# Attention and feed-forward stack on one core: a list scheduler in place of hand-written time tables, with other score, softmax and norm steps

## The chip, the cores and the metric

The kernel runs on one NeuronCore of a Trainium2 chip. The metric is device time in microseconds: the median of three runs. The profile is one further execution, taken by the hardware profiler. The engines are PE (TensorE; PEld is its weight load), DVE (VectorE), ACT (ScalarE), POOL (GpSimd) and SP (SyncE, which here issues DMAs).

## What is computed

The input x holds 32 batch elements of 128 tokens by 128 channels, all in float32. First comes one cross attention with a residual, then a layer norm, then six layers of local attention and gated feed forward; the sum of the two residual streams is the output. Shortened from the reference:

```
x = x + xattn(layernorm(x), ctx, ...)          # 16 heads of 8, 4 key/value groups, time bias
y = layernorm(x)
for i in range(6):
    # attention: 16 heads of 64; queries and keys are normalised per head, then rotated
    q, k, v = split(shift_tokens(y) @ Wqkv[i])
    q, k = rotate(l2norm(q) * qs), rotate(l2norm(k) * ks)
    y = local_attention(q, k, v) @ Wo[i] + y    # windows of 32, each sees itself and the one before
    # feed forward: layer norm, 341 hidden columns, gelu gate
    t = layernorm(shift_tokens(y)) * g + b
    a, gate = split(t @ W1[i] + b1[i])
    y = (a * gelu(gate)) @ W2[i] + b2[i] + y
return x + y
```

`shift_tokens` delays the upper 64 channels by one token. `layernorm` and `l2norm` need a reciprocal square root per row.

## The kernel before

All activations stay on the chip. Four batch elements form a group (8 groups); one batch element in one layer is a **unit** (192 units). Products that must be precise are made from operands split into a high and a low part, three matmuls into one PSUM bank (`split3`, lines 636 to 638).

A unit makes four 512-wide query and key products (`pqk`). From each bank ScalarE takes squares (line 686), VectorE sums them per head (line 689), and VectorE multiplies the bank by two rotation tables (two instructions, line 694); GpSimd adds the two with halves swapped (line 700). One reciprocal square root over all 32 heads follows: a floor, logarithm and exponential on ScalarE (lines 126, 128), and a Newton step of three instructions; the floor (line 118) and the Newton step (lines 133, 135, 137) run on VectorE. GpSimd applies it (line 723). PE transposes the result (line 729); ScalarE, and VectorE for a part (line 744), copy it out, keys into tiles `kb` whose other half is zero, so that two heads share one matmul over all 128 rows.

Values are multiplied by the product of value and output weights (`py`); ScalarE copies them out (line 762) and four DMAs per product (line 769, 16 a unit) regroup them by window into `ysh`. Scores start with a matmul that writes the mask into the bank (line 781), then 32 logical matmuls (line 786; each is two in the trace). VectorE takes row maxima (line 793). ScalarE makes 16 exponentials of 64 columns a unit, each with its own bias and a sum of its row (line 804; the sum is read out by a second instruction). GpSimd divides (line 813), VectorE transposes in blocks (line 817), and 28 logical matmuls multiply by `ysh` (line 830; 56 in the trace).

Per group: the input is transposed, with a shifting matmul for the upper half (lines 660, 661), and split (lines 666, 670). After attention come a residual, a DMA that shifts the upper half (line 851), statistics in eight instructions of 64 (lines 857, 858), a reciprocal square root on VectorE and ScalarE (lines 116 to 137), and normalising in two GpSimd passes (lines 867, 868 and 880). Then come a transpose, the gate and value products, gelu, their product (line 928), the second product (line 935) and a residual (line 939).

In cross attention each batch element has four groups of heads: scores (line 516), sum with the bias and maximum on VectorE (line 522), subtraction on GpSimd (line 526), exponential (line 530), transposes (line 416), copies (line 537), and one value product per group into a strip of 32 rows (line 542).

What sets the order is written out by hand. Every step is pushed into a heap with a time, and the heap is emptied in order of time; each engine then runs its instructions in that order. The times are the tables `OFF`, `GOFF`, `OFF1` and `GOFF1` times a slot, the same for every group. PSUM has five banks for products, two for scores and one for outputs.

Of the kernel before, what the change touches and what calls it, by code (L numbers as in the profile page):

```python
# [22 lines left out]
NRT = 8  # L23
NYT = 4
NKB = 3
NQT = 3
EWD = (1,)
STORE = 0.4
MP1 = [23.0 + 1.2 * i for i in range(8)]
WV1, DH1, DL1 = [20.85, 22.05], 0.15, 0.3  # L30
PREP0, PREPT = 10.0, 7.0
SHIFT = 6.0
FFT = 7.0
MP = [31.47, 31.72, 31.97, 32.22, 32.47, 32.72, 32.97, 33.22]
WV, BIAS, DH, DL = [24.4, 25.4], 16.4, 0.06, 0.14
T1 = 7.0
NI1 = 180
OFF1 = dict(
    sc=[[0, 2, 26, 28], [32, 34, 73, 75], [93, 95, 139, 141], [154, 159, 170, 172]],
    mx=[[1, 3, 27, 29], [33, 35, 74, 76], [94, 96, 140, 142], [158, 164, 171, 173]],  # L40
    sb=[[4, 5, 30, 31], [36, 37, 77, 78], [97, 98, 143, 144], [165, 168, 174, 175]],
    ex=[[39, 41, 44, 48], [99, 100, 101, 102], [151, 152, 155, 160], [187, 189, 192, 196]],
    tp=[[42, 46, 51, 55], [126, 127, 128, 129], [153, 157, 163, 167], [190, 194, 199, 203]],
    st=[[45, 50, 54, 57], [130, 132, 134, 135], [156, 162, 178, 179], [193, 198, 202, 205]],
    pa=[[49, 53, 82, 83], [131, 133, 136, 137], [161, 166, 186, 188], [197, 201, 218, 220]],
    oT=[[84], [138], [191], [223]], pb=[[145], [146], [195], [227]], rl=[[147], [148], [200], [232]],
    at=[[149], [150], [204], [236]],
)
GOFF1 = dict(
    ldc=[-101], gst=[-121, -120], gr0=[-119], gr1=[-117, -116], gr2=[-115, -114, -113], xa=[-118], xb=[-112],  # L50
    px=[-89], pxe=[-88], pcx=[-100], pce=[-99], pk=[-77], ke=[-76], kd=[-75], pq=[-74, -73, -71, -67],
    qe=[-72, -69, -65, -62], qd=[-70, -66, -63, -60], pv=[-55], vt=[-11], td=[-110], ab=[-109, -108], ln=[-4],
    mkb=[-56], tbm=[-3], p2=[238], aT=[249], pw=[265], rs=[266], hst=[267, 268], hr0=[269], hr1=[292, 296],
    hr2=[299, 301, 302], xf1=[270], xf2=[303],
)
T = 13.3
NI = 331
OFF = dict(
    qk=[[0, 1, 30, 31], [79, 80, 107, 108], [153, 154, 194, 195], [244, 245, 284, 285]],
    sq=[[2, 6, 32, 36], [81, 85, 109, 113], [155, 159, 196, 200], [246, 250, 286, 290]],  # L60
    ss=[[7, 11, 37, 41], [86, 90, 114, 118], [160, 164, 201, 205], [251, 255, 291, 295]],
    ta=[[3, 8, 33, 38], [82, 87, 110, 115], [156, 161, 197, 202], [247, 252, 287, 292]],
    tb=[[4, 9, 34, 39], [83, 88, 111, 116], [157, 162, 198, 203], [248, 253, 288, 293]],
    add=[[5, 10, 35, 40], [84, 89, 112, 117], [158, 163, 199, 204], [249, 254, 289, 294]],
    rs0=[[42], [119], [206], [296]], rs1=[[62, 63], [141, 142], [219, 220], [313, 314]],
    rs2=[[64, 65, 66], [143, 144, 145], [221, 222, 223], [315, 316, 317]],
    mul=[[67, 68, 69, 70], [146, 147, 148, 149], [224, 225, 226, 227], [318, 319, 320, 321]],
    tq=[[100, 102, 104, 136], [181, 183, 185, 228], [268, 270, 272, 275], [354, 356, 358, 381]],
# [15 lines left out]
)  # L84

@with_exitstack
def body(ctx: ExitStack, tc: tile.TileContext, x, ctx_in, fside, mask, xWq, xWk, xWv, xWo, xtw,
         Wqkv, q_scale, k_scale, Wo, ln_g, ln_b, W1, b1, W2, b2, cst, x1d, out):
    nc = tc.nc
    B = x.shape[0]  # L90
# [265 lines left out]
    def attn_ops(g, j, G):  # L356
# [26 lines left out]
        def rs1(c):  # L383
            rsqrt_b(G["rsq"], c)
# [651 lines left out]
```

## Time and profile before

| | us |
|---|---|
| median of three runs | 3325.82 |
| lowest and highest | 3324.84, 3329.13 |
| span of the profiled execution | 3320.9 |

The granted TensorE clock of the profiled execution averages 0.994. Busy time of an engine is the union of its instructions. In lists of groups, a row gives the line, engine, operation, tiles, shapes and count, then busy microseconds and the mean nanoseconds of one, then the engine's idle time before these instructions and what ended it. More rows of that list:

| line | engine, what | count | busy us | mean ns |
|---|---|---|---|---|
| 118 | DVE floor of the per-unit norm | 192 | 164.6 | 857 |
| 133 | DVE first Newton product, per unit | 192 | 94.2 | 491 |
| 135 | DVE second, per unit | 192 | 50.6 | 264 |
| 137 | DVE third, per unit | 192 | 36.9 | 192 |
| 116 | DVE epsilon of the feed-forward norm | 48 | 36.2 | 755 |
| 133 | DVE first Newton product of that norm | 48 | 9.1 | 190 |
| 137 | DVE third Newton product of that norm | 48 | 18.5 | 386 |
| 857, 858 | DVE statistics of 64 columns | 384 | 79.3 | 207 |
| 700 | POOL addition of the rotation | 768 | 980.3 | 1286 |
| 723 | POOL product with the norm | 768 | 777.4 | 1043 |
| 867, 868 | POOL subtraction of the mean | 96 | 59.2 | 616 |
| 880 | POOL product with the feed-forward norm | 48 | 50.0 | 1041 |
| 735 | ACT copy of 128x512 from PSUM | 384 | 208.1 | 590 |
| 739, 746 | ACT copies of 64x512 from PSUM | 576 | 336.9 | 585 |
| 781 | PE mask into the score bank | 384 | 148.7 | 387 |
| 786 | PE scores | 12288 | 375.1 | 262 |
| 660, 661 | PE input transposes and shifts | 576 | 139.3 | 296 |
| 885 | PE transposes for the feed forward | 192 | 30.9 | 284 |

### The profile page before, as it was taken

To read this page: it belongs to the slowest core of one execution; us is meant where nothing else is said; L and a number is where in the kernel's file an instruction comes from. 1 tells how busy PE (TensorE), PEld (TensorE's weight loads), DVE (VectorE), ACT (ScalarE), POOL (GpSimd) and SP (SyncE) were. 2 spreads that over 40 slices of the span, in tenths; PEclk is the share of its full clock that TensorE was granted. 3 is DMA by queue.
4 is the path that set the end of the run, shared out by engine and by line. 5 is a ranking of instruction groups with operands and counts; after the bars stand their busy time and mean duration, and the time that the engine had idled before them with its cause. 6 is when DMAs were issued, how large, how long until landed. Compare 5 with 4: busy or idle time off the path is not lost.

```text
span 3320.9 us, 102077 instructions
## 1 busy us (share of the span) xinstructions
PE 3155.8 (95%) x35979; PEld 2389.3 (72%) x35979; DVE 2979.5 (90%) x6954; ACT 2834.9 (85%) x9983; POOL 2468.3 (74%) x2284
## 2 busy tenths in 40 slices
PE   8999899999999999999999999999999999999997
PEld 5555677777777777777777777777777777777775
DVE  6666899999999999999999998998999998999995
ACT  6776888898888898889898889898888898898895
POOL 5655777777787777787787787786787776777873
PEclk9999999999999999999999999999999999999998
DMA  2110333332333332233332333332333332333332
GB/s 61 33 37 12 77 87 82 79 74 71 75 83 86 78 74 72 72 85 84 77 77 71 75 83 81 79 77 68 79 83 76 84 76 64 77 82 81 82 83 62
DMA packets 217966, 243.80 MB, mean 73 GB/s; under 512 B 83534, under 2 KB 112498, under 8 KB 217458
## 3 DMA queue, kind: packets, MB, share of 16 engines
q1 hardware_dynamic: 217026, 236.93, 28.8%
q8 instruction: 288, 4.72, 0.6%
q14 instruction: 220, 1.80, 0.2%
q10 hardware_dynamic: 432, 0.34, 0.0%
HBM read 25.31 MB, written 4.19 MB: 9 GB/s over the span
## 4 chain that ended last, share of the span: by engine, by line
PE 49%; DVE 32%; ACT 8%; issue 4%; DMA 3%; SPq 2%; POOL 1%; ACTq 0%; DVEq 0%; POOLq 0%
DVE t L694 10%; PE pO L830 8%; PE ptq L729 7%; DVE ss L689 6%; PE sc L786 4%; DVE rnv L118 3%; PE pa L542 3%; PE pqk L636 3%; PE pqk L638 3%; ACT pr L804 3%; PE pqk L637 3%; DVE mx L793 2%; DVE PT L817 2%; SPq L769 2%; PE py L636 2%
## 5 line engine op out<-in xcount | busy, mean ns | idle before, releaser
L700 POOL TENSOR_TENSOR rt<-t,t 128x512 f32<-128x512 f32 x768 | 980.3, 1286 | 372.8 <-DVE t L694 330.8
L694 DVE TENSOR_TENSOR t<-pqk,tab 128x512 f32<-128x512 f32 x1536 | 983.3, 681 | 115.9 <-ACT sq L686 110.3
L804 ACT ACTIVATE pr<-sc,mx 128x64 f32<-128x64 f32 x3072 | 915.7, 331 | 61.2 <-DVE PT L817 53.0
L723 POOL TENSOR_TENSOR rt<-rt,rny 128x512 f32<-128x512 f32 x768 | 777.4, 1043 | 214.1 <-DVE rny L137 213.4
L804 ACT ACTIVATION_READ_ACCUMULATOR pr<-sc,mx 128x1 f32 x3072 | 691.9, 225 | 0.0
L689 DVE TENSOR_REDUCE ss<-sq 128x8 f32<-128x512 f32 x768 | 517.4, 674 | 0.0
L830 PE MATMUL pO<-ysh,PT 128*32 128x128 f32 x10752 | 416.9, 275 | 53.3 <-DVE PT L817 48.7
L813 POOL TENSOR_TENSOR pr<-pr,rl 128x512 f32<-128x512 f32 x384 | 400.8, 1044 | 89.2 <-DVE rl L809 89.2
L686 ACT ACTIVATE sq<-pqk 128x512 f32<-128x512 f32 x768 | 429.3, 600 | 24.6 <-PE pqk L638 12.5
L830 PEld LDWEIGHTS pO<-ysh,PT 128*32 128x32 f32 x10752 | 367.1, 110 | 97.6 <-DVE PT L817 72.1
L762 ACT COPY yt<-py 128x512 f32<-128x512 f32 x768 | 416.8, 614 | 21.2 <-PE py L638 17.2
L729 PE MATMUL ptq<-cs,rt 128*128 128x128 f32 x3072 | 409.8, 278 | 22.2 <-DVE t L694 17.0
L729 PEld LDWEIGHTS ptq<-cs,rt 128*128 128x128 f32 x3072 | 334.5, 141 | 96.7 <-issue 52.5
L786 PE MATMUL sc<-kb,qT 128*32 128x128 f32 (+1 forms) x12288 | 375.1, 262 | 15.2 <-DVE kb L744 14.8
L786 PEld LDWEIGHTS sc<-kb,qT 128*32 128x32 f32 x12288 | 270.7, 109 | 114.5 <-issue 70.7
L636 PE MATMUL py<-mw,xsh 128*128 128x512 f32 x768 | 333.1, 434 | 8.9 <-ACT yt L762 5.8
L636 PE MATMUL pqk<-wqh,xsh 128*128 128x512 f32 x768 | 314.0, 409 | 4.8 <-ACT yt L762 2.8
L638 PE MATMUL py<-mw,xsl 128*128 128x512 f32 x768 | 301.9, 393 | 0.0
L638 PE MATMUL pqk<-wqh,xsl 128*128 128x512 f32 x768 | 300.9, 392 | 0.0
L637 PE MATMUL pqk<-wql,xsh 128*128 128x512 f32 x768 | 300.8, 392 | 0.0
L637 PE MATMUL py<-mw,xsh 128*128 128x512 f32 x768 | 300.6, 391 | 0.0
L735 ACT COPY qT<-ptq 128x512 f32<-128x512 f32 x384 | 208.1, 590 | 79.0 <-PE ptq L729 78.1
(168 smaller groups left out, 5756.8 us busy)
## 6 DMA issues: line engine op xcount, KB each, us to landing
ysh<-yt SPq DMA_DIRECT2D x3072, 64.0 KB
raw<-in_L_ffn_Wqkv SPq DMA_DIRECT2D x36, 256.0 KB
xsu<-xt SPq DMA_DIRECT2D x48, 127.0 KB
wor<-in_L_ffn_Wo SPq DMA_DIRECT2D x6, 512.0 KB
xt<-in_x SPq DMA_DIRECT2D x8, 256.0 KB
cx<-in_ctx SPq DMA_DIRECT2D x8, 256.0 KB
mk<-in_mask_BxS_ff SPq DMA_DIRECT2D x8, 256.0 KB
x_scratch<-xt SPq DMA_DIRECT2D x8, 256.0 KB
```

The lines of the kernel that those rows point to most:

```text
L636: nc.tensor.matmul(pt, lh, rh, start=True, stop=False)
L637: nc.tensor.matmul(pt, lh, rl, start=False, stop=False)
L638: nc.tensor.matmul(pt, ll, rh, start=False, stop=True)
L686: nc.scalar.activation(V["sq", c], V["pp", c], AF.Square)
L689: nc.vector.tensor_reduce(V["ss"][:, c * 8:(c + 1) * 8], V["sq", c].rearrange("p (h d) -> p h d", d=64), axis=AX.X, op=ALU.add)
L694: nc.vector.tensor_tensor(V["t", k, c].rearrange("p h s d -> p h (s d)"), V["pp", c].rearrange("p (h d) -> p h d", d=64), w["tab"][:, c // ...
L700: nc.gpsimd.tensor_tensor(V["rt", c], V["t", 0, c], V["t", 1, c][:, :, ::-1, :], op=ALU.add)
L723: nc.gpsimd.tensor_tensor(rv, rv, V["rn"][:, c * 8:(c + 1) * 8].unsqueeze(2).to_broadcast([P, 8, 64]), op=ALU.mult)
L729: nc.tensor.transpose(V["ptq", c][:, k, :], V["rt", c][:, 2 * k:2 * k + 2].rearrange("p h s d -> p (h s d)"), ident)
L786: nc.tensor.matmul(sc[32 * c:32 * c + 32, :, wd, lo:64], qT[:, c, 32 * wd:32 * wd + 32], kT[:, c, :, 32 * wd - 32 + lo:32 * wd + 32], star ...
L804: nc.scalar.activation(pr[:, q, :], scv[:, q, :], AF.Exp, bias=mx[:, q:q + 1], accum_out=ls[:, q:q + 1])
L830: nc.tensor.matmul(pO[32 * wd:32 * wd + 32, j, :], PT[:, half, wd, blk, :], ysh[u][:, (2 * par + half) * P:(2 * par + half + 1) * P], star ...
```

## The change

The whole body is rewritten around a list scheduler; the mathematics stays the same.

- **Order.** `Sched.op` records a step with its engine (from `COST`), the buffers that it reads and writes, and a priority: the unit's position, plus a correction by name (`LATER`). `Sched.run` plays these steps through with the two durations of `COST` (how long the engine is taken, when the result is there): at each moment each engine takes the ready step of the highest priority whose buffers are free; some steps must leave PSUM banks free (`KEEP`). The instructions are then issued in that order. Cross attention has priorities before those of layer 0. Some pools of buffers hand out their buffers in the order of the program.
- **Scores.** Keys and queries keep both heads of a pair in one tile. Each head has its own matmul over 64 rows, into one of two banks by the half of the rows: 64 logical matmuls, of 32 output rows by 64 columns (32 in the first window). The mask comes into each bank as a ScalarE copy.
- **Softmax.** The negative maxima are added into the bank by one matmul with the identity and a broadcast operand (`fold`); then come one exponential of 512 a bank without bias, a row-sum reduction on VectorE, and the rest as before.
- **Rotation.** One VectorE product of 1024 with both tables replaces two of 512.
- **Norms.** The per-unit floor and Newton step are on VectorE. The epsilon and the Newton step of the layer norms are on GpSimd, in four instructions after the exponential. Normalising in the feed forward is four VectorE instructions with two per-row scalars.
- **Shift.** x is kept with a shifted copy of its upper half beside it, renewed by two DMAs after each residual. Input transposes read it, without shifting matmuls; statistics are four instructions of 128.
- **Cross attention.** The four value products of a batch element are issued together.
- **Value products of a unit** are issued together, once both halves of the softmax are there.

```
-OFF = dict(
-    qk=[[0, 1, 30, 31], [79, 80, 107, 108], [153, 154, 194, 195], [244, 245, 284, 285]],
...
-    def drain():
-        while heap:
-            _, _, fn, a = heapq.heappop(heap)
-            fn(*a)
+COST = dict(
+    ax=("PE", .46, .7), axh=("ACT", .51, .62), axl=("DVE", .60, .68),
...
+    def run(self):
...
+                for o in cand[e]:
+                    if o.ready > t + 1e-9:
+                        continue
+                    if o.table == "E" and hold:
+                        continue
...
+                cand[e].remove(o)
...
+                free[e] = t + occ
...
+        for (_, o), new in zip(order, fresh):
...
+            o.fn()
...
-                nc.tensor.matmul(sc.rearrange("p a b c -> p (a b c)"), identb, maskb, start=True, stop=True)
...
-                for c in range(4):
-                    nc.tensor.matmul(sc[32 * c:32 * c + 32, :, wd, lo:64], qT[:, c, 32 * wd:32 * wd + 32],
-                                     kT[:, c, :, 32 * wd - 32 + lo:32 * wd + 32], start=False, stop=True,
-                                     skip_group_check=True)
+                    for c in range(4):
+                        for a in range(2):
+                            r = slice(64 * a, 64 * a + 64)
+                            nc.tensor.matmul(s4[a][32 * c:32 * c + 32, half, wd, lo:64],
+                                             q[r, c * P + 32 * wd:c * P + 32 * wd + 32],
+                                             k[r, c * P + 32 * wd - 32 + lo:c * P + 32 * wd + 32], start=False, stop=True,
+                                             skip_group_check=True)
+        for a, b in enumerate(sc):
+            S.op("msk", lambda b=b: nc.scalar.copy(b.t, mask), pri, (), [b], k=a)
+        S.op("sc", scores, pri, [*qT, *sc], sc)
...
-            for q in range(4 * half, 4 * half + 4):
-                nc.scalar.activation(pr[:, q, :], scv[:, q, :], AF.Exp, bias=mx[:, q:q + 1],
-                                     accum_out=ls[:, q:q + 1])
+            S.op("fold", lambda: nc.tensor.matmul(s.t, identr, mx.t.unsqueeze(2).to_broadcast([P, 8, 64]), start=False,
+                                                  stop=True, skip_group_check=True), pri, [mx, s], [s], k=a)
+            S.op("ex", lambda: nc.scalar.activation(pr.t, s.t, AF.Exp), pri, [s], [pr], table="E", k=a)
+            S.op("sm", lambda: nc.vector.tensor_reduce(sm.t, r8(pr), axis=AX.X, op=ALU.add), pri, [pr], [sm], k=a)
...
-            nc.vector.tensor_tensor(V["t", k, c].rearrange("p h s d -> p h (s d)"),
-                                    V["pp", c].rearrange("p (h d) -> p h d", d=64),
-                                    w["tab"][:, c // 2, k, :].unsqueeze(1).to_broadcast([P, 8, 64]), op=ALU.mult)
+                nc.vector.tensor_tensor(t.t.rearrange("p (k h d) -> p k h d", k=2, d=64),
+                                        bc(pp.t.rearrange("p (h d) -> p h d", d=64), 2),
+                                        tab.t[:, c // 2].unsqueeze(2).to_broadcast([P, 2, 8, 64]), op=ALU.mult)
...
+        small = NW == "dve" and floor is not None
+        e = nc.vector if small else nc.gpsimd
...
+                    nc.vector.tensor_scalar(xn.t[:, k * P:(k + 1) * P], xsg(g)[:, k], mv.t[:, k, 0:1], r.t[:, k:k + 1],
+                                            op0=ALU.subtract, op1=ALU.mult)
...
+            nc.sync.dma_start(xt[g][1:113, :, 128:192], xt[g][0:112, :, 0:64])
+            nc.sync.dma_start(xt[g][113:P, :, 128:192], xt[g][112:P - 1, :, 0:64])
...
+        def xpa():
+            for h in range(4):
+                nc.tensor.matmul(pa.t[32 * h:32 * h + 32, :], v.t[:, j, h, :], sts[h].t, start=True, stop=True)
```

## The prediction

> **What bounds the kernel now.** I read the busy times first, then the stages, then VectorE's waits, then rows.
>
> ```profile
> PE 3155.8 (95%) x35979; PEld 2389.3 (72%) x35979; DVE 2979.5 (90%) x6954; ACT 2834.9 (85%) x9983; POOL 2468.3 (74%) x2284
> PE 49%; DVE 32%; ACT 8%; issue 4%; DMA 3%; SPq 2%; POOL 1%; ACTq 0%; DVEq 0%; POOLq 0%
> ```
>
> No engine is alone at its limit, and the chain of waits changes hands between PE and DVE, so the shares must be read by stage. The columns of the stage view are start:end, length, then busy time and instructions of PE, PEld, DVE, ACT and POOL. The first two lines are cross attention and one whole layer; the third is that layer again with line 830 alone (columns PE and PEld).
>
> ```profile
> 40.00:300.00 260.00, 247.17 (x1589) 144.38 (x1588) 172.99 (x1177) 185.12 (x376) 148.94 (x142) 1.00 0.11 31
> 1326.40:1820.70 494.30, 476.22 (x5704) 369.06 (x5701) 462.31 (x933) 437.23 (x1594) 381.05 (x351) 1.00 0.32 78
> 1326.40:1820.70 494.30, 68.80 (x1795) 60.64 (x1792) 1.00 0.32 78
> ```
>
> A unit (one batch element in one layer) issues 56 matmuls at line 830, so 1792 are 32 units: 494.3 / 32 = 15.45 us a unit, and 192 x 15.45 = 2966 us. The first query matmul of layer 0 starts at 299.5 us in the timeline. Of the span of 3320.9 us, 300 is thus cross attention, 2966 the layers, and 55 filling and draining. PE's 96% in a layer counts the modelled ends of pipelined matmuls; VectorE, in order, is busy 462.3 / 494.3 = 93.5%, 14.45 us a unit. I take it as the bound of the layers. Its idle 32.0 us of that layer:
>
> ```profile
> DVE t L694 <- ACT sq L686: 16.9, 24, 2.8
> DVE u L928 <- PE pa L638: 5.0, 14, 0.4
> ```
>
> Half of the idle time ends on ScalarE, which is itself busy 437.2 / 494.3 = 88%. Some of VectorE's busy time is no work:
>
> ```profile
> 1502.53 1.29 POOL L700 TENSOR_TENSOR rt<-t,t 128x512 f32<-128x512 f32 x1 [0.49 <-PE ptq L729]
> 1503.01 0.84 DVE L118 TENSOR_SCALAR rnv<-ss 128x32 f32<-128x32 f32 x1
> 1503.77 0.19 DVE L809 RECIPROCAL rl<-ls 128x8 f32<-128x8 f32 x1
> ```
>
> The 32-element step of line 118 takes 0.84 us and ends where the GpSimd instruction ends (1503.82). Its shortest instance takes 0.235. Such steps, SBUF to SBUF on VectorE, sit out a running GpSimd instruction.
>
> **The change, by engine, per unit of a layer.** The rows (count over the execution | busy us, mean ns):
>
> ```profile
> L694 DVE TENSOR_TENSOR t<-pqk,tab 128x512 f32<-128x512 f32 x1536 | 983.3, 681 | 115.9 <-ACT sq L686 110.3 <-POOL pr L813 1.6 <-POOL rt L700 0.9
> L689 DVE TENSOR_REDUCE ss<-sq 128x8 f32<-128x512 f32 x768 | 517.4, 674 | 0.0
> L744 DVE COPY kb<-ptq 64x512 f32<-64x512 f32 x192 | 133.4, 695 | 7.0 <-ACT kb L739 1.0
> L135 DVE SCALAR_TENSOR_TENSOR frt<-frv,frt 128x4 f32<-128x4 f32 x48 | 43.8, 912 | 1.6
> L804 ACT ACTIVATE pr<-sc,mx 128x64 f32<-128x64 f32 x3072 | 915.7, 331 | 61.2 <-DVE PT L817 53.0 <-DVE mx L793 0.9
> ```
>
> *VectorE.* Two products of 512 become one of 1024: now 8 x 0.64 = 5.12 us. The 128-wide score step of line 522 (0.286) and the 512-wide one here (0.681) give 1.03 ns an element, so 4 x (0.64 + 512 x 1.03 ns) = 4.67: -0.45. The copy of line 744 goes: -0.70. The row sums that ScalarE's accumulator made become two reductions like line 689: +2 x 0.674 = +1.35. The four steps of the feed-forward norm (36.2 + 9.1 + 43.8 + 18.5 = 107.6 us over 192 units) leave for GpSimd: -0.56. Eight statistics steps of 64 (79.3 us) become four of 128 (0.280 each, line 374): 0.28 - 0.41 = -0.13. Normalising comes from GpSimd as four steps of 128x128 a group; line 334 has that shape at 0.223 with GpSimd idle: 4 x 0.223 / 4 = 0.22. Their wait for GpSimd is not in this trace. Least is none; most is a whole 1.29 us addition each, 1.29 a unit. The nearest row is the old norm: four steps, 107.6 / 48 = 2.24 us a group; the shortest of lines 116, 133 and 137 are 0.17, 0.12 and 0.16, and with 0.16 for the fourth, work is 0.6, so 1.64 of waits a group, 0.41 a unit, which I take: +0.63 in all. The per-unit norm is on VectorE before (lines 118 to 137, 346 us, 1.80 a unit) and after: 0, at best -1.0 (their shortest instances, 0.235 + 0.146 + 0.191 + 0.191 = 0.76), at worst +0.45 (as long as the old norm's 2.24). Sum: 14.45 - 0.45 - 0.70 + 1.35 - 0.56 - 0.13 + 0.63 = **14.59 us**, from 13.1 to 15.9. VectorE's load hardly moves.
>
> The Trainium skill (SBUF — State Buffer, "SBUF: two separate sides") makes this wait a lock on a port pair held for a whole instruction, also against VectorE instructions in a two-port mode. By it all four normalising steps lose what is left of an addition; at a whole one each VectorE would carry 15.47 us a unit and, filled like my forecast, the kernel would take 3372 us. The row of the old norm, with 0.41 us per step lost on average (1.64 / 4), says 3198.
>
> *ScalarE.* 16 exponentials of 64 with their accumulator reads go: they start some 0.29 apart in the timeline, -4.6. Two of 512 (line 530, 0.628) and two mask copies (line 735, 0.59) come: +2.44. Five evacuations of transposes become four: -0.48. 13.66 becomes 11.0: the largest relief, off VectorE's chain except where VectorE waited for the square.
>
> *PE.* The mask matmuls go, 148.7 / 192 = -0.77; two 512-wide folds come, 0.23 each by the start times of lines 637 and 638 (1502.92, 1503.15): +0.46. Input transposes lose the shifting matmuls: (83.1 + 56.2 - 30.9) / 192 = -0.56. Scores: 64 matmuls (1.95 us) become 128, half as tall, half as wide. The timeline up to 1509.18 and up to 1509.31:
>
> ```profile
> 1509.15 0.26 PE L786 MATMUL sc<-kb,qT 128*32 128x64 f32 x4
> 1509.15 0.43 PE L786 MATMUL sc<-kb,qT 128*32 128x64 f32 x12
> ```
>
> Four column strips start together and the next four 64-wide ones 0.065 us on. If the row halves overlap too: 16 x 0.065 + 0.27 = 1.3 us. If not: 32 x 0.065 + 0.27 = 2.35. I take 1.8. PE: 14.88 falls by 1.5 to 0.5; at my value to 13.9, below VectorE either way.
>
> A rule of the Trainium skill (TensorE: Matmul & The Clock Gate, "Wait — 56ns, not 53.3ns?") speaks against this: matmul starts are never nearer than about 25 ns, however narrow. By it 128 cost 3.2 us, PE 15.26 a unit, 15.73 at the same fill, and the kernel 3330 us instead of 3198. But the row has eight starts in 0.13 us, 16 ns each, so across strips the row decides.
>
> *GpSimd.* 381.1 / 32 = 11.9; two normalising passes go (50.0 + 59.2 us, -0.57), five tiny steps a group come (fills of 128x16 and 128x128 take 0.12 and 0.21: at most +0.26): 11.6. The norm now queues behind 1.0 to 1.3 us instructions; VectorE's normalising and all tables queued behind it wait for that. The other seven groups are the cover; without it up to four such instructions a group, 1.3 a unit.
>
> *SP and buffers.* 16 moves of values a unit stay (10.0 us of issue in the timeline). The shift becomes four issues a group where there was one of 0.76: +0.57 a unit, below 15. The second shift feeds the next layer, 28 units on: nothing. A unit now takes both score banks from mask copy to exponential, about 6 us; the qT slots serve one unit at a time, about 5: cover is the rest of the unit.
>
> *Cross attention.* PE is busiest, 247 of 260:
>
> ```profile
> L542 PE MATMUL pa<-ST,v 128*32 128x512 f32 x232 | 83.7, 605 | 11.9 <-ACT ST L537 11.9
> ```
>
> Eight a batch element: 83.7 / 29 = 2.9 us. Together in four strips, about 1.0; 1.9 x 29 = 55 us less, PE 192. At 90% of PE that is 213 us for 260: -47. Nothing if ScalarE's and VectorE's waits replace it; -68 if PE ran solid. I take -50.
>
> **Sum.** The square's wait (16.9 of 494.3) goes with ScalarE's relief; the other 15.1 stay, so VectorE is 97% busy: 14.59 / 0.97 = 15.04 a unit. 250 + 55 + 192 x 15.04 = 3193 us of span. The median of the runs is 3325.8, 5 above the span: **3198 us**, 3.8% less.
>
> **Rivals.**
> - *Port waits mostly vanish.* The order is no longer periodic, so line 118 need not meet an addition each time. For: line 135's per-unit steps mostly run at 0.19. Against: GpSimd stays 77% busy. VectorE falls to 13.1 and PE, at the middle of 13.4 and 13.9, is the larger: 13.6 / 0.97 = 14.0, so 305 + 2688 + 5 = 2998 us.
> - *Port waits take over: slower.* The four normalising steps and the longer per-unit norm lose whole additions, and VectorE's queue stands behind GpSimd's norm. VectorE 15.9 / 0.97 = 16.4: 305 + 3149 + 5 = 3459 us. It decides from 15.7 a unit on ((3321 - 305) / 192). For: line 135 in the old norm loses 0.7 nearly every time. Against: four fewer such steps in that norm.
> - *The new order does not do what a denser one would.* Fill stays 93.5%: 15.60 a unit, 305 + 2995 + 5 = 3305 us. For: costs are fixed ahead of time, and port waits are not among them. Against: ScalarE is no longer near its limit.
>
> **From these to numbers.** Forecast 0.46 (its own range 3110 to 3280), vanish 0.16, take over 0.28, same fill 0.10. The time is the forecast's. The range of 3000 to 3390 leaves out the lowest of the second and the top half of the third, about 0.2. A change within 0.2% (7 us) can't be told from none: 0.04, from the edges of the last two. Slower 0.28; faster 0.68.
>
> **What will show it.** Cross attention ending near 250 us; VectorE near 97% in a layer with the wait for the square gone; ScalarE near 73%; scores at 1.3 to 2.35 us a unit. Line 118's successor far above 1 us, or the 128x128 normalising steps near 1 us each, would prove the slow rival. I am wrong on the bound if VectorE falls below 90% while PE stays near its present share.

## The result, and the profile after

The changed kernel takes 3449.9 us (median of 4, 3446.8 to 3452.0) against 3325.3 for the kernel before on the same chip: a ratio of 1.0374, 95% interval 1.0359 to 1.0389. Forecast were 3198 us, in a range of 3000 to 3390. It is 3.7% slower where 3.8% faster was predicted.

From the page of the changed kernel (its span is 3448.4 us), the busy times and the chain of waits by engine:

```profile
PE 3113.7 (90%) x47887; PEld 2404.7 (70%) x47887; DVE 2917.7 (85%) x6115; ACT 2227.7 (65%) x4415; POOL 2413.6 (70%) x2470
PE 34%; DVE 26%; DMA 11%; SPq 11%; ACT 10%; issue 6%; POOL 2%; ACTq 0%; POOLq 0%; DVEq 0%
```

VectorE's busy time fell a little (the forecast had it hardly move), and so did every engine's share: time is lost with no engine at work harder. And the chain has a new part: DMA and SP's queue are 22% of it, 5% before.

The windows of the changed kernel (columns as in the prediction; the last three are the granted TensorE clock, the share of DMA and GB/s): cross attention, a layer (layer 4), and two stretches of 52 us at the end of layer 0:

```profile
40.00:300.00 260.00, 214.34 (x1473) 141.25 (x1471) 152.47 (x988) 176.07 (x349) 139.35 (x170) 0.90 0.13 35
2441.40:2944.20 502.80, 470.60 (x7684) 371.15 (x7684) 452.13 (x803) 334.42 (x663) 368.60 (x366) 0.99 0.32 79
838.00:890.00 52.00, 42.47 (x769) 31.82 (x768) 49.88 (x91) 28.46 (x62) 41.64 (x42) 0.94 0.18 45
890.00:942.00 52.00, 41.98 (x412) 32.10 (x411) 31.00 (x49) 24.06 (x45) 26.05 (x24) 0.86 0.25 64
```

Cross attention did get lighter (PE 214 of 260 us where it was 247) but not shorter: ScalarE's exponentials (line 724) wait 47 us of that window for GpSimd's subtraction (line 722). In layer 4 VectorE carries 452.1 / 32 = 14.13 us a unit, yet the unit takes 15.71, so it is busy 89.9% and not 97%; PE is busy 94%, where it was 96%. That is the sign which the prediction had set for being wrong on the bound. And at the end of layer 0 VectorE works 60% of a stretch in which nothing else is at its limit.

I read the stages by the start of the first PV product (line 830 before, 913 after) of a unit:

| | first PV product | us a unit, layers 0 to 5 | profiled span |
|---|---|---|---|
| before | 355.9 | 15.3, 15.44, 15.45, 15.43, 15.44, 14.9 | 3320.9 |
| after | 367.9 | 15.9, 16.71, 16.85, 15.75, 15.75, 14.9 | 3448.4 |

(Each layer is taken from the start of its predecessor's last unit to the start of its own last, so the gap at the end of layer 0 falls in the second figure.)

So there are three losses against the forecast: a late start (+12 us where -50 was forecast), gaps at the ends of layers 0 and 1, and regular units of 15.7 us where 15.04 was forecast.

**The gap.** From last PV product to last PV product, the four units across the end of layer 0 take 108.7 us, those across the end of layer 1 108.4; across later ends 66 to 72. In these lines of the changed kernel's trace, the columns of a source view are line, engine, operation, tiles, count, shortest/median/longest ns, and first and last start. First the last three of the five copies of value products (line 851) from 836 to 905 us, then the matmuls that build the next layer's value weights (line 562):

```profile
L851 ACT COPY yt__11845<-bank__61 x1: 607/607/607, 848.5 to 848.5; 128x512 f32<-128x512 f32 x1
L851 ACT COPY yt__11866<-bank__64 x1: 586/586/586, 849.6 to 849.6; 128x512 f32<-128x512 f32 x1
L851 ACT COPY yt__11903<-bank__62 x1: 647/647/647, 852.5 to 852.5; 128x512 f32<-128x512 f32 x1
...
L562 PE MATMUL bank__64<-stg__1904,stg__1905 x8: 272/396/507, 853.3 to 901.5; 64*128 64x128 f32 x8
...
L562 PE MATMUL bank__63<-stg__1904,stg__1905 x4: 272/272/373, 898.4 to 898.9; 64*128 64x128 f32 x4
```

After 852.5 no value product is copied until 906.4. The weights that they need are built by 32 matmuls, of which 4 run at 853 us and the next at 898: in the scheduler this step (`mp`) may start only when it leaves two of the five PSUM banks free (`KEEP`, mp=2), so three have to be free at once. PV products of successive units start at 860.0 and 919.7.

**SP's queue.** The chain of waits of the changed kernel in a regular part (start, us, what; its longest pieces):

```profile
2608.10 0.51 ACT bank__67 L884
2608.61 0.33 SPq L861
2608.99 0.59 SPq L861
2609.62 0.59 SPq L861
2610.25 1.99 DMA ysh__39327<-yt__39466
2612.38 1.91 PE bank__68 L913 x50
```

A value block has been copied out, and its four moves are issued one by one by SP, 0.59 us each and more for some; the last lands about 2 us later, and the PV products (line 913) go on when it has. From first start to last start the PV products of a unit take 2.28 us (median) where they take 1.7 undisturbed, and 48 us of PE's idle time in the run end on such a move (4.4 in the kernel before). What the new order lacks is lead: from the end of a unit's last issue to the start of its first PV product pass 1.1 us (median of units 41 to 180), less than a move needs to land, where the old order left 6.8.

SP's queue works in order. In the waits of SP in layer 4, a shift (line 752) stands first in the list, and whatever moves come after it wait behind it:

```profile
SPq L752 <- DVE sm__43415 L896: 15.8, 1, 15.8
SPq L861 <- ACT bank__67 L884: 12.4, 2, 11.3
SPq L752 <- DVE sm__40385 L896: 11.7, 1, 11.7
```

SP issues 11.56 us a unit in that layer (10.25 before), and for much of the rest it stands at a source that is not ready: 34 us of the layer at a shift's, 108 at a move's. That alone does not make it the bound, since before it stood longer, 191 us of a layer.

### The profile page after: what moved, and what is told of

It is laid out like the page before. It is cut to its first block, busy times and chain, and to the rows that moved or that the text cites. A ratio compares the mean times of both kernels' runs of the same rounds, so it can differ in the third digit from the quotient of the medians.

```text
span 3448.4 us, 118846 instructions
## 1 busy us (share of the span) xinstructions
PE 3113.7 (90%) x47887; PEld 2404.7 (70%) x47887; DVE 2917.7 (85%) x6115; ACT 2227.7 (65%) x4415; POOL 2413.6 (70%) x2470
## 4 chain that ended last, share of the span: by engine, by line
PE 34%; DVE 26%; DMA 11%; SPq 11%; ACT 10%; issue 6%; POOL 2%; ACTq 0%; POOLq 0%; DVEq 0%
SPq L861 10%; PE bank__68 L913 7%; DMA xt<-xt 2%; PE bank__66 L879 2%; PE bank__64 L441 1%; PE bank__67 L879 1%; PE bank__63 L441 1%; PE bank__61 L441 1%; PE bank__65 L441 1%; PE bank__63 L435 1%; PE bank__62 L435 1%; PE bank__62 L441 1%; PE bank__65 L435 1%; PE bank__61 L435 1%; PE bank__63 L436 1%
## 5 line engine op out<-in xcount | busy, mean ns | idle before, releaser
L884 ACT COPY bank__66<-mask 128x512 f32<-128x512 f32 x192 | 117.0, 610 | 5.7 <-PE bank__66 L362 4.4
L884 ACT COPY bank__67<-mask 128x512 f32<-128x512 f32 x192 | 116.5, 607 | 1.5 <-PE bank__67 L362 1.1
L724 ACT ACTIVATE ysh__88<-ysh__88 128x512 f32<-128x512 f32 x96 | 60.7, 634 | 57.0 <-POOL ysh__88 L722 56.9
L921 DVE TENSOR_TENSOR xt<-bank__68,xt 128x512 f32<-128x512 f32 x48 | 33.0, 687 | 16.7 <-PE bank__68 L913 16.5
L441 PE MATMUL bank__61<-cs,ysh__88 128*128 128x128 f32 x84 | 15.5, 315 | 10.2 <-ACT ysh__88 L724 10.2
L441 PE MATMUL bank__63<-cs,ysh__88 128*128 128x128 f32 x80 | 14.6, 312 | 10.8 <-ACT ysh__88 L724 10.5
L441 PEld LDWEIGHTS bank__63<-cs,ysh__88 128*128 128x128 f32 x80 | 9.9, 156 | 15.0 <-ACT ysh__88 L724 12.8
L441 PEld LDWEIGHTS bank__61<-cs,ysh__88 128*128 128x128 f32 x84 | 10.9, 160 | 13.6 <-ACT ysh__88 L724 12.2
L441 PE MATMUL bank__62<-cs,ysh__88 128*128 128x128 f32 x76 | 14.5, 324 | 5.6 <-ACT ysh__88 L724 5.4
L441 PE MATMUL bank__64<-cs,ysh__88 128*128 128x128 f32 x68 | 12.7, 318 | 7.6 <-ACT ysh__88 L724 7.5
L441 PE MATMUL bank__65<-cs,ysh__88 128*128 128x128 f32 x76 | 13.3, 302 | 6.4 <-ACT ysh__88 L724 6.1
L441 PEld LDWEIGHTS bank__62<-cs,ysh__88 128*128 128x128 f32 x76 | 10.7, 168 | 8.4 <-ACT ysh__88 L724 7.6
L695 DVE TENSOR_TENSOR xt<-bank__68,xt 128x512 f32<-128x512 f32 x8 | 5.5, 685 | 12.8 <-PE bank__68 L693 12.8
L441 PEld LDWEIGHTS bank__64<-cs,ysh__88 128*128 128x128 f32 x68 | 8.6, 159 | 10.9 <-ACT ysh__88 L724 10.2
L441 PEld LDWEIGHTS bank__65<-cs,ysh__88 128*128 128x128 f32 x76 | 9.5, 154 | 9.5 <-ACT ysh__88 L724 8.7
L727 ACT COPY ysh__88<-bank__63 128x512 f32<-128x512 f32 x20 | 11.9, 597 | 1.8 <-PE bank__63 L441 1.6
L727 ACT COPY ysh__88<-bank__61 128x512 f32<-128x512 f32 x21 | 12.3, 586 | 1.2 <-PE bank__61 L441 1.1
```

Source lines behind the costliest of these rows:

```text
L441: nc.tensor.transpose(dst[:, k * P:(k + 1) * P], srcs[k], ident)
L724: S.op("xex", lambda: nc.scalar.activation(sm.t, sm.t, AF.Exp), pri, [sm], [sm], table="E")
L727: S.op("xev", lambda: nc.scalar.copy(sm.t, pt.t), pri, [pt, sm], [sm])
L884: S.op("msk", lambda b=b: nc.scalar.copy(b.t, mask), pri, (), [b], k=a)
L921: S.op("res", lambda: nc.vector.tensor_tensor(xv(g), hv(po.t), xv(g), op=ALU.add), pri, [po, X[g]], [X[g]])
```

## Experiments

Each is set against the kernel before on the same chip, and its ratio is given with its 95% interval. "The plan" is the list of start times that the scheduler itself works out from its table of costs.

**The gaps and the late start**

e1: `KEEP` mp=2 becomes mp=0.

```
-KEEP = dict(... wvp=2, mp=2, bip=2, ...)
+KEEP = dict(... wvp=2, mp=0, bip=2, ...)
```

> The changed kernel, with no PSUM bank kept free for the steps mp of the weight preparation (they asked for two more than their own). Theory, gaps in the order: the schedule itself, played through with its own costs, has 99.9 and 98.9 us for the last four units of layers 0 and 1 where other fours take some 56, because mp waits for three free banks; without the reserve its length falls from 3146 to 3101 us, so the time falls by about 45 us from 3450, to 3405, and the last fours of layers 0 and 1 drop from 108 us to below 75. Rival, that the gaps come from weights arriving late on the chip: the time stays within 15 us and the long fours stay.

3378.4 us, ratio 1.0159 (1.0143 to 1.0174): 71 us less than the changed kernel. The units of layers 1 and 2 fall from 16.71 and 16.85 to 16.01 and 15.46. The gaps are the bank rule's doing in this order, and cost more than the plan says.

e2: cross attention gets ten score buffers, four of them lent by tiles that the layers use later.

```
-lent = [borrow("nh", 0), borrow("xh", 1), borrow("xl", 1), borrow("ysh", 1)]
+lent = [borrow("nh", 0), borrow("xh", 1), borrow("xl", 1), borrow("ysh", 1), borrow("nl", 0)]
+lent += [borrow("u", i) for i in range(3)]
...
+           + [b.t for b in lent[4:]])
```

> The changed kernel with ten buffers for the scores of cross attention instead of six (four tiles of the feed forward are lent to it, as four others already are). Theory, buffers: the joint value product holds all four score buffers of a batch element until the fourth is ready, and six buffers serve one and a half elements; with ten the first value product of layer 0 ends near 330 us instead of 371 and the whole takes about 85 us less, 3365. Rival, that cross attention is bound by the work of PE or by GpSimd's subtraction in its chain: first value product within 15 us of 371, time above 3420.

3359.0 us, 1.0099 (1.0084 to 1.0115), 91 us less. The first PV product comes at 340.3, 28 us earlier, and one of the two gaps closed with the other order. Joint value products hold four score tiles until the last is ready; with six tiles there were not enough to begin the next batch element.

e5: e2, and the step before `mp` (`wvp`) freed of the bank rule; `mp` keeps it.

```
-KEEP = dict(... wvp=2, mp=2, bip=2, ...)
+KEEP = dict(... wvp=0, mp=2, bip=2, ...)
```

> The changed kernel with ten score buffers in cross attention and with the weight products of the next layer (wvp) no longer required to leave two PSUM banks free (KEEP wvp 2 to 0). The scheduler's own plan is 123.4 us shorter than the changed kernel's (3022.2 against 3145.6) and has no gap left at any layer end (14.21 us a unit in four layers running); the first value product stands 42.7 us earlier in it. Theory (the loss is the plan's: a late start and gaps at the ends of layers): the real time falls by 110 to 160 us, to 3290 to 3340, so at or a little below the kernel before; the real layers run at 15.2 to 15.6 us a unit, none above 15.8. Rival (the gaps only gather waits that the ports and the late moves cause anyway): the time stays above 3350, and the units inside the layers become longer than 15.6 us.

3314.1 us, 0.9975 (0.9959 to 0.9992), 136 us less. No gap is left, though `mp` still has its rule: all 32 weight matmuls run from 793 to 815 us. So which of the two rules opens a gap depends on the order that surrounds it. The regular units stay at 15.5: the layers have no gain over the kernel before, only the start has.

e12: e5 with the four value products of cross attention one by one.

```
-            for h in range(4):
-                nc.tensor.matmul(pa.t[32 * h:32 * h + 32, :], v.t[:, j, h, :], sts[h].t, start=True, stop=True)
-        S.op("xpa", xpa, pri, [v, *sts, *lent[1:]], [pa], also=[oT])
+        for h in range(4):
+            S.op("xpa1", lambda h=h: nc.tensor.matmul(...), pri, [v, sts[h], *lent[1:]], [pa], also=[oT])
```

> The version of e5 with the four value products of a batch element in cross attention issued one by one, each when its own scores are ready, in place of all four together. The plan's first value product of layer 0 stands at 376.9 us in place of 300.1, and its length is 3101 in place of 3022. Theory (the joint products are a gain of the size that the prediction gave, 50 us, as soon as they have buffers for their four score tiles): the first PV product comes 50 to 75 us later than e5's 333.7, and the time is 50 to 80 us longer, 3365 to 3395. Rival (the products cost nothing alone, since PE starts narrow ones side by side in both): within 20 us of e5's 3314.

3378.9 us, 1.0159 (1.0144 to 1.0174), 65 us more than e5; the first PV product comes at 396.0 against 333.7. With buffers enough, the joint products are worth 62 us. (The granted clock in the window of cross attention was 1.00 before, 0.90 in the changed kernel, 0.95 in e5 and 1.00 in e12. It does not order the starts: e12 has the full clock and the latest start.)

**Which engine paces the layers**

e3 and e4: the floor and the Newton step of the per-unit norm left out, in the changed kernel and in the one before.

```
-        S.op(names[0], f0, pri, [src], [v])
+        S.op(names[0], (lambda: None) if small else f0, pri, [src], [v])
...
+        if small:
+            f3 = f4 = f5 = lambda: None
```

> The changed kernel in its own order, but the floor and the three Newton instructions of the per-unit norm are left out on VectorE (the norm is then the exponential alone). They take 1.29 us a unit, of which some 0.5 is waiting for GpSimd. Theory, port waits and VectorE's load set the pace: the units lose about 1.3 us each, 250 us in all, 3200 us. Rival, the order and its waits set the pace whatever VectorE does: less than 100 us, above 3350.

3406.6 us, 1.0245 (1.0221 to 1.0269): 43 us less.

> The kernel before, with the same four per-unit norm instructions left out (1.80 us a unit there). Theory, VectorE's load sets the pace of the layers before the change: 192 x 1.8 = 345 us less, 2980 us. Rival, PE and ScalarE in the hand-written order set it: less than 120 us, above 3200. In between, the three engines share the bound.

3214.7 us, 0.9668 (0.9652 to 0.9684): 111 us less, 14.88 us a unit. The same relief of VectorE, or one somewhat larger (1.80 us a unit before, 1.29 after), gives 111 us before and 43 after.

e11: the same in e5.

> The version of e5 with the floor and the Newton step of the per-unit norm (four VectorE instructions a unit, 1.29 us a unit with their waits for the port) left out, same order. Theory (PE sets the pace): the time falls by less than 60 us, above 3255. Rival (VectorE sets the pace once the gaps are closed): at least 0.9 us a unit, 170 us, to 3145 or less.

3302.0 us, 0.9929 (0.9913 to 0.9946): 12 us less. VectorE does not pace the layers once the gaps are closed.

e9 and e10: the third matmul of each split product left out, before and in e5.

```
         nc.tensor.matmul(pt, lh, rh, start=True, stop=False)
-        nc.tensor.matmul(pt, lh, rl, start=False, stop=False)
-        nc.tensor.matmul(pt, ll, rh, start=False, stop=True)
+        nc.tensor.matmul(pt, lh, rl, start=False, stop=True)
```

> The kernel before with the third matmul of each split product (low part of the left side times high part of the right) left out; the order is the same. PE loses 9.5 matmuls of 0.235 us a unit, 2.3 us of 14.9. By the prediction's reading (VectorE bounds the layers and PE follows it): the time stays within 25 us of 3323, above all the cross attention's share of it. Rival (PE's own 14.9 us of 15.45 set the pace as much as VectorE's 14.45): VectorE alone would then be the bound, at 14.45 / 0.97 = 14.9 us a unit, 0.55 less, so the time falls by 80 to 130 us, to 3195 to 3245.

3331.8 us, 1.0017 (1.0006 to 1.0029): nothing gained. PE, 96% busy by the records of before, paces nothing there.

> The version of e5 (ten score buffers, wvp 0; changed kernel without gaps, 15.5 us a unit) with the third matmul of each split product left out, same order. PE loses 2.3 to 2.45 us a unit of its 14.4 us. Theory (once the gaps are closed, PE's work, 14.4 us and not the 13.9 that the prediction had, sets the pace of the layers): VectorE's 14.2 us becomes the bound, 14.6 to 14.9 us a unit, and the time falls by 110 to 170 us, to 3145 to 3205. Rival (late moves, port waits and a fixed order set the pace, none of them PE's): the time falls by less than 50 us.

3292.2 us, 0.9888 (0.9860 to 0.9916): 22 us less, where the theory wanted 110 to 170. My theory that PE's work sets the pace fell.

e7: ScalarE relieved in the kernel before.

```
-            for q in range(4 * half, 4 * half + 4):
-                nc.scalar.activation(pr[:, q, :], scv[:, q, :], AF.Exp, bias=mx[:, q:q + 1], accum_out=ls[:, q:q + 1])
+            if half == 0:
+                nc.scalar.activation(pr, scv, AF.Exp, scale=0.0, bias=mx[:, 0:1])
```

> The kernel before with ScalarE relieved: of the softmax, the sixteen exponentials a unit with their row sums (8.4 us of ScalarE a unit by the rows of before) are left out, and two wide ones with scale 0 stand in for them; the row sums are a constant. By the prediction's step that the fill rises when the wait for ScalarE's square goes (0.55 us a unit over 192 units) the time falls by about 105 us, to some 3220. Rival (VectorE's idle time in the kernel before is spread over waits that take each other's place, so that relieving one engine which is not the busiest gives little): 3295 to 3330.

3278.3 us, 0.9866 (0.9853 to 0.9878): 45 us less, 15.20 us a unit. It fits neither, since its premise fails: the square's wait did not go. In the same stretch of 494.3 us ScalarE's busy time fell from 437 to 335 us, and VectorE still waits for the square (line 694 of the kernel before, 696 here), 15.1 us where it was 16.9:

```profile
DVE t L696 <- ACT sq L688: 15.1, 25, 2.8
```

So ScalarE's load is not what that wait hangs on. Of VectorE's 32.0 us of idle time in that stretch 6.6 went, about half of them in its waits at line 928.

e8: the per-unit norm's steps on GpSimd.

```
-NW = "dve"
+NW = "pool"
```

> The changed kernel with the floor and Newton step of the per-unit norms on GpSimd, in four instructions of GpSimd after the exponential, in place of VectorE's. The plan is 23 us shorter (3122). VectorE's port waits of these steps (1.29 us a unit against 0.71 in the plan) go, and GpSimd gets about 1.6 us a unit more. Theory (the changed kernel is paced by its plan and by PE, VectorE's waits are bridged): the time changes by the plan's 23 us, 3410 to 3450. Rival (VectorE's waits for the port set the pace): VectorE loses 1.29 us a unit, 248 us over the run, of which at least half shows: below 3330.

3380.6 us, 1.0171 (1.0158 to 1.0185): 69 us less, between the two. The scheduler makes another order for it, so how much is the order and how much the port stays open; e11 says that these steps cost e5 no more than 12 us.

**SP's queue**

e6: values shifted by way of DRAM, 6 transfers a unit in place of 16.

```
-YD = "sb"
+YD = "dram"
```

> The changed kernel with its shifted values sent through DRAM: 6 transfers a unit on SP's queue in place of 16. The plan is 40.5 us shorter (3105.1). Theory (SP's issues, 0.67 us each and 76% of its time, make the last value moves late, and the PV products wait 51 us for them over the run): the waits of the PV products for DMA fall below 15 us, SP is busy under 45%, and the time falls by the plan's 40 us and some of the 51, to 3360 to 3410. Rival (the way through DRAM is longer in itself, so the products wait more): the waits for DMA grow over 80 us and the time is not below 3450.

4638.9 us, 1.396 (1.394 to 1.398). The rival's side, and far beyond it. In SP's timeline of that kernel a read back (line 856) is issued 7.9 us after the last write of its pair (line 853, second line), and both wait in the one queue:

```profile
2011.28 0.90 SPq L853 DMA_DIRECT2D y_scratch<-yt__22232  x1
2013.16 0.51 SPq L853 DMA_DIRECT2D y_scratch<-yt__22268  x1
2021.07 0.62 SPq L856 DMA_DIRECT2D ysh__22144<-y_scratch  x1
2021.79 0.52 SPq L853 DMA_DIRECT2D y_scratch<-yt__22384  x1
```

The write shown after the read goes out only when the read has left. As a test of the issue cost it tells nothing, since it puts a longer wait in the same place; e13 was made for that.

e13: e5 with half the moves left out, at the same order.

```
-  S.op("dm", lambda u=u: nc.sync.dma_start(...), pri, [yt], ysh, k=c)
+  S.op("dm", lambda u=u: u < 2 and nc.sync.dma_start(...), pri, [yt], ysh, k=c)
```

> The version of e5 with 8 of the 16 value moves a unit left out (the last two of each four; their places hold zeros from the start), same order on every engine. SP's queue loses 8 x 0.67 = 5.3 us a unit of its 11.8 (in e5 it is busy 76% of a layer, and for much of the rest it waits, in order, for the shifts' and the moves' sources). Theory (SP's queue, by now, sets the pace of the layers: moves issue late, PV products wait, and what follows on PE with them): the layers fall from 15.5 to 14.9 us a unit or less, the time by 100 us or more, to 3215 or less. Rival (the PV products' waits for moves are only the place where other lateness shows): less than 40 us, above 3275.

3207.1 us, 0.9645 (0.9632 to 0.9658): 107 us less than e5, 15.03 us a unit (14.9 or less was expected). The chain of waits and the busy times of 500 us of its layers:

```profile
DVE 45%; PE 38%; issue 7%; ACT 4%; POOL 3%; DMA 2%; SPq 1%; POOLq 0%; DVEq 0%; ACTq 0%
1700.00:2200.00 500.00, 469.84 (x7979) 376.56 (x7972) 472.34 (x842) 348.72 (x695) 386.41 (x387) 0.99 0.20 48
```

DMA and SP's queue leave the chain (20% in e5, 3% here), VectorE heads it, busy 94.5%. The last move of a unit is now issued 5.7 us before its first PV product (1.2 in e5). This is the state that the prediction had in mind. Half of the bytes went with the issues here; e18 below keeps all of them.

e15: e13 and e10 together.

> The version of e5 with both the half of the moves (e13) and the third matmul of each split product (e10) left out. e10 alone gave 22 us. Theory (SP's queue sets the pace and hides PE's): once SP is relieved PE's 2.4 us a unit show too, and the time is at least 60 us under that of e13. Rival (neither): within 40 us of e10's 3292.

3165.9 us, 0.9522 (0.9507 to 0.9536): 41 us below e13, where at least 60 was expected of PE as the hidden second bound. PE's 2.4 us a unit give 0.1 us with SP's queue in the way and 0.2 without.

e16 and e17: half the moves left out of the kernel before and of the changed one.

```
-            for u in range(4):
+            for u in range(2):
...
-                                         ysh[u][:, (2 * par + half) * P:(2 * par + half + 1) * P],
+                                         ysh[u % 2][:, (2 * par + half) * P:(2 * par + half + 1) * P],
```

> The kernel before with 8 of its 16 value moves a unit left out (two of each four; the PV products read the two tiles that are filled, so two of the four 32-row blocks of values are the wrong ones). SP's queue loses 8 x 0.61 = 4.9 us a unit of its 10.2. Theory (the change made SP's queue a bound; before, it was none: 2% of the chain of waits, PV products wait 2 us for moves in the whole run): within 20 us of 3324. Rival (the queue paced the layers before too): 60 us or more faster.

3308.3 us, 0.9949 (0.9932 to 0.9965): 17 us less.

> The changed kernel itself with 8 of its 16 value moves a unit left out as in e13 (zeros in their place), same order, the gaps at the ends of layers 0 and 1 kept. Theory (SP's queue costs some 0.45 us a unit in every layer, gaps are a second loss beside it): layers 2 to 4, 15.77, 15.71 and 14.98 us a unit, fall by 0.4 to 0.7 each, the ends of layers 0 and 1 keep a group over 90 us, and the time is 80 to 130 us less, 3320 to 3370. Rival (the gaps are the queue's work too): 190 us or more less, below 3260.

3321.7 us, 0.9990 (0.9981 to 0.9999): 128 us less. The later layers run at 15.04, 15.05 and 14.17 us a unit; the four units across the ends of layers 0 and 1 still take 104.5 and 101.2 us. So the queue's part and the gaps' part stand side by side, and the queue was no bound before.

e14 and e18: every fourth move issued by ScalarE, in an order that the scheduler makes for it with moves at 0.67 us (e14), and at e5's order (e18).

```
-  S.op("dm", lambda u=u: nc.sync.dma_start(...), pri, [yt], ysh, k=c)
+  S.op("dm", lambda u=u: (nc.scalar if u == 3 else nc.sync).dma_start(...), pri, [yt], ysh, k=c)
```

> The version of e5 with every fourth value move issued from ScalarE's queue in place of SP's, and the price of a move in the scheduler set to 0.67 us in place of 0.62, as the trace shows it. Nothing is left out. SP loses 4 x 0.67 = 2.7 us a unit; ScalarE, 67% busy, gets 4 x 0.42 = 1.7 us by the one row of its own issues (0.42 us). The plan is 53 us shorter than that of e5 with moves at 0.67 (3053 against 3106). Theory (SP's queue sets the pace): 30 to 90 us faster than e5's 3314, to 3225 to 3285. Rival (ScalarE's stream is the worse place, or SP is no bound): 3300 to 3400.

3347.2 us, 1.0064 (1.0052 to 1.0077): DMA and SP's queue are down to 7% of the chain, and the time is 33 us over e5's. The PV products of a unit start within 1.68 us (median), so moves no longer hold them up. What in the new order costs the time is not settled.

> The version of e5 with every fourth value move issued by ScalarE, the order of everything else as in e5 (in e14 the scheduler had made another order for it). Nothing is left out. SP's queue falls from 11.6 to 9.0 us a unit; ScalarE, 10.4 us a unit, gets four issues of 0.54 us, as measured in e14. Theory (SP's queue sets the pace): half of what e13 gave, 40 to 70 us under e5's 3314, to 3245 to 3275. Rival (an issue in ScalarE's stream holds up the squares and exponentials behind it as much as it frees SP): 3305 or more.

3234.0 us, 0.9732 (0.9718 to 0.9747): **the best version, complete, 2.7% under the kernel before and 6.3% under the changed one.** It is 80 us under e5, more than expected. Busy times and chain of its page, and a layer:

```profile
PE 3008.9 (93%) x47887; PEld 2373.2 (73%) x47887; DVE 2921.4 (90%) x6115; ACT 2230.0 (69%) x4415; POOL 2415.7 (75%) x2470
DVE 41%; PE 37%; ACT 7%; issue 6%; DMA 5%; SPq 2%; POOL 1%; ACTq 0%; DVEq 0%; POOLq 0%
1768.70:2258.80 490.10, 458.08 (x7696) 366.81 (x7688) 456.78 (x804) 335.86 (x666) 370.45 (x368) 0.99 0.33 81
```

SP issues 9.0 us a unit in that layer, in place of 11.5; the last issue of a unit comes 3.0 us before its first PV product (1.2 in e5), and 4.5 us of PE's idle time in the whole run end on a move (29 in e5). All the bytes still move, so it was the issuing from one queue, not the transfers, that held the PV products up. The Trainium skill (Perfetto Trace Analysis, "DMA Optimizations") says that balancing DMAs over the engines that can issue them may help where making descriptors is the bottleneck. e18 agrees with 80 us; e14, the same split in another order, has 33 us against it.

## Why the prediction was wrong

**The loads were mostly right, their setting was not.** By the prediction's own steps, per unit:

| term | predicted | measured (layer 4 of the changed kernel) |
|---|---|---|
| VectorE | 14.59 | 14.13 |
| of it, normalising with waits | 0.63 | 0.77 |
| of it, per-unit norm | 1.80 | 1.29 |
| ScalarE | 11.0 | 334.4 / 32 = 10.45 |
| GpSimd | 11.6 | 368.6 / 32 = 11.52 |
| PE | 13.9 | 470.6 / 32 = 14.71 |
| scores on PE, up to the next start | 1.8 (1.3 to 2.35) | 1.53 |
| SP, issue | 10.0 + 0.57 | 11.56 |
| fill of VectorE | 97% | 90% |

PE is the one load that was mis-sized against the change. The mask (-0.64), the folds (+0.54), the scores (-0.29) and the input transposes (-0.40) came near their terms; but the PV products went from 2.08 to 2.40 and the split products from 6.96 to 7.34 (busy time up to the next start), which no term had. e10 and e15 show that this load costs little (0.1 to 0.2 us a unit for 2.4).

**The step that failed** is in the sum: "The square's wait (16.9 of 494.3) goes with ScalarE's relief; the other 15.1 stay, so VectorE is 97% busy". Neither half held. ScalarE was relieved, and the wait stayed: 15.9 us in layer 4 of the changed kernel (lines 793 and 816 on line 787, summed over their tiles), and 15.1 in e7, where the old order was kept. And the other idle time grew: VectorE is idle 50.5 us of layer 4, of which 10 end on PV products and 5 on the shift's transfer. The step took the waits of the old order over into a new one. Three terms were missing, each with a measured size:

- *SP's queue, +128 us (e17).* The prediction costed it, "+0.57 a unit, below 15. The second shift feeds the next layer, 28 units on: nothing", and let a queue below its limit pass as free. But the new order issues a unit's last move only 1.1 us ahead of its PV products, and a move takes 2 us to land, so the issues in front of it show in the time. Before, with 6.8 us of lead, the same half of the moves is worth 17 us (e16). How much of the 128 the added shifts cause is open: no run took them away.
- *Gaps at the ends of two layers, some 80 us.* Twice 108 us for four units in place of 66 to 72; e1 got 71 back. The prediction took the layers as 192 equal units and never asked which bank rule the step to the next layer meets.
- *The late start, 62 us.* Forecast was a first PV product 50 us before the old 355.9, measured is 367.9. The joint products have the worth that the prediction gave them (62 us in e12) with ten score buffers; with six the gain went into ScalarE's wait. The prediction named it ("Nothing if ScalarE's and VectorE's waits replace it") and gave it no weight. Ten buffers bring 34 of the 62 us back (e5); where the other 28 go is open.

128 + 80 + 62 = 270 against the 252 us between 3198 and 3450; they overlap a little. The other way round, e13, without gaps, with ten buffers and with half of the moves left out, takes 3207 us at 15.03 a unit, where the prediction has 3198 at 15.04. In part that is luck: VectorE's load is lower there and its fill 94.5%, not 97%.

**What bounded the kernel before** was read rightly in the main. VectorE's relief gave 111 us (e4), PE's nothing (e9), SP's 17 (e16), ScalarE's 45 (e7). But VectorE's bound is soft: of 1.80 us a unit taken away only 0.57 showed in the time.

**The rivals.** "Port waits take over" gave 3459 us, within 10 of the result, and is wrong all the same. VectorE's port waits are there: four normalising steps of 128x128 take 4.03 us while GpSimd runs additions of 1.26 to 1.34 us back to back.

```profile
2200.86 4.03 DVE L939 TENSOR_SCALAR sq__32938<-xt,nmv__32810,ny__32830 128x128 f32<-128x128 f32 x4
...
2200.99 1.34 POOL L809 TENSOR_TENSOR rt__32672<-t__32898 128x512 f32<-128x512 f32 x1
2202.30 1.28 POOL L809 TENSOR_TENSOR rt__32709<-t__32846 128x512 f32<-128x512 f32 x1
2203.54 1.26 POOL L809 TENSOR_TENSOR rt__32818<-t__32889 128x512 f32<-128x512 f32 x1
```

This agrees with the lock that the Trainium skill tells of (SBUF — State Buffer, "SBUF: two separate sides"). But VectorE's load did not grow to that rival's 15.9: it is 14.13, with 0.77 for these steps and their waits; and taking the per-unit norm's steps away gives 43 us in the changed kernel and 12 in e5. "Port waits mostly vanish" had the direction of the load (13.1; the forecast's own 14.59 is nearer) and missed the rest. Nearest in mechanism is the third, "the new order does not do what a denser one would", with costs fixed ahead of time; it stopped at the old fill of 93.5%, as if an order could not be worse than the old one.

## What to carry to other kernels

Busy shares price a change only as long as the order stays; where a planner makes a new order, look first at what it must wait for by its own rules (free banks, buffers held until the last of a group) at the places where one layer gives way to the next. Cost an in-order queue by how long before its consumer the last entry goes out, not by its sum alone: SP was busy 66% of a layer and nearly harmless with 6.8 us of lead, and 74% and a pace-setter with 1.1. And a time that matches a rival's does not prove its mechanism: relieving the suspected engine tests it, and here that gave 43 us of the 125 between the two kernels, and 12 once the gaps and the late start were mended.

## What the runs showed of the hardware

**Narrow matmuls can start 6 to 8 ns apart** where they go to different column strips and row halves. The timeline of scores in the changed kernel (line 879):

```profile
780.45 0.21 PE L879 MATMUL bank__67<-qT__10641,qT__10618 64*32 64x32 f32 x1
780.46 0.21 PE L879 MATMUL bank__66<-qT__10641,qT__10618 64*32 64x32 f32 x1
780.46 0.21 PE L879 MATMUL bank__67<-qT__10641,qT__10618 64*32 64x32 f32 x1
780.47 0.21 PE L879 MATMUL bank__66<-qT__10641,qT__10618 64*32 64x32 f32 x1
```

All 128 of a unit take 1.35 us from first to last start (median), 10.6 ns from one to the next on average, and 1.56 us to the last one's end, within the prediction's bounds. The floor of about 25 ns between starts that the prediction weighed from the Trainium skill (TensorE: Matmul & The Clock Gate, "Wait — 56ns, not 53.3ns?") is not seen here; by an estimate from that figure the 128 would have taken 3.2 us.

**An issue of a move by SP** takes 0.59 us (median in layer 4 of the changed kernel), 0.66 on average there, and 2.05 at the longest. With half of the moves left out the mean is 0.60 (e13, 500 us of its layers; 0.65 in e5). On ScalarE a move's issue takes 0.52 us (mean in the layer of e18).
